# Four images on one core: where images 1 to 3 are loaded, normalised and laid out as a pixel table

## The chip, the cores and the metric

The kernel runs on one core of a Trainium2 chip. A core has a matrix engine (PE, whose weight loads are shown apart as PEld), a vector engine (DVE), an activation engine (ACT), a general engine (POOL) and a sequencer for transfers (SP). Each works through its own list of instructions in order and waits for the others by semaphores. Transfers (DMAs) are issued from the lists of SP, ACT and POOL; all share the core's 16 DMA engines. The metric is the time of one execution on the device in microseconds (us): 4742.62 us before the change, the median of three runs (4736.29 to 4742.63). All data are 32-bit floats.

## The reference, cut to what matters

The input `x` has four images of 32 by 32 pixels and 384 channels. Four layers follow each other, each a residual on a group-normalised input:

```python
x = x + _L0_conv_ref(_gn(x), ...)   # deformable attention, 6 heads of 64 channels
x = x + _L1_conv_ref(_gn(x), ...)   # attention, 12 heads of 32 channels, reweighted by a similarity
x = x + _L2_conv_ref(_gn(x))        # ratio of box sums
x = x + _L3_conv_ref(_gn(x), ...)   # outlook attention, 3 x 3 neighbourhoods
```

`_gn` takes the mean and variance of each image over groups of 12 channels and all 1024 pixels. Layer 0 projects the normalised image to queries, runs a grouped 3 x 3 convolution over them, turns its result into one sampling position for each pixel and head group, and samples the same normalised image bilinearly at these positions: four neighbouring pixels, weighted. The samples give keys and values; the logits also get a bias, sampled from a table around each position. No image depends on another.

## The kernel before

**Two lanes.** `Front` does layer 0 of an image, `Trunk` does layers 1 to 3. Image 0's front comes first, alone. Then the trunk of image b runs beside the front of image b + 1, and the trunk of image 3 runs alone. Both lanes are Python generators that emit instructions and yield a number of steps. `Net.layer3` mixes them: after each yield of the trunk it lets the front go on until its share is `LEAD` = 0.1 ahead of the trunk's. A trunk counts 1109 steps (`TRUNK_STEPS`), a front 714 (`FRONT_STEPS`). A front therefore ends when its trunk has done nine tenths, and the next front begins beside the last part of that trunk, the normalisation and products of its layer 3 (L1634 and on). A planner then puts the instructions of each engine in order from its own estimates of when each can start; what is emitted late can be placed early. Instructions under `pin` (`keep_in_program_order`) keep the order of the program.

**The first part of a front** is `normed(b)` (L544). It loads the image's pixels (`xin`, four DMAs of 384 KB on SP, L550), transposes them to channels on PE (24 transposes, L560) with eight copies on ACT (L565), stores the transposed image `x0` (one DMA of 1.5 MB on ACT's list, L568; `outputs0` reads it back at L457 for the residual), normalises it (`norm_steps`, L322: six statistics and three means on DVE, 28 one-column products with `gmat` on PE at L338, a square root on ACT at L361, three scalings on DVE at L369), transposes it back (24 transposes, L583; eight copies into `xn` on ACT, L589, two buffers) and stores every 128 pixels twice into the pixel table `pairs` in DRAM (16 DMAs of 192 KB on SP, L591), from which the bilinear samples are gathered (L707). `xin`, `x`, and the normalised `xh` share two buffers of one tag, `a12`. For image 0, `normed` also issues `borders` (L232, zeros at the edges of every pixel table, four DMAs for each on ACT's list) and `windows` (the bias tables, up to the six stores of `strips` at L193, also on ACT's list).

After `normed`, `inputs0` makes queries (`w_q`, 36 matmuls at L388, read back at L618), the convolution (216 matmuls, L637, read back at L645), layer norm and positions on DVE, the gathers and the keys and values. Then come the heads.

**Image 0's heads** (`heads0`) are a row of 96 blocks (6 heads, 2 halves of the queries, 8 key tiles) written out by hand as a software pipeline, with nearly everything pinned. A turn `t` runs from -3 to 118. Beside these turns the kernel already does one piece of another image: `early0` runs `normed(1)` and stores `xh` as `xh1` in DRAM. `normed(1)` yields in small pieces (30 in all, the flag `alone`), and one piece is taken after each turn from t = 17. So image 1's front starts from `xh1` and the finished table (L601 to L610), while images 2 and 3 call `normed` at the head of their own fronts, beside the trunks of images 0 and 1, in two lumps: up to the normalisation, and the pixel table.

**Buffers in DRAM**: two pixel tables and two `x0`, taken in turn by `b % 2`; one `xh1`.

Of the kernel before, what the change touches and what calls it, by code (L numbers as in the profile page):

```python
# [26 lines left out]
P = 128  # L27
NB, HW, C = 4, 32, 384
N = HW * HW
KC = C // P  # L30
NJ = N // P
G, GC = 6, 64
# [26 lines left out]

TRUNK_STEPS, FRONT_STEPS, LEAD = 1109.0, 714.0, 0.1


def bc(ap, axis, n):
# [7 lines left out]
class Net:  # L73
# [121 lines left out]
    def scratch(self):  # L195

        self.pairs = []
        for i in range(2):
            t = self.dram.tile([G * SLOTS, 2 * GC], F32, tag=f"pairs{i}", name=f"pairs{i}")
            self.pairs.append(t)  # L200
        dram = lambda name, shape: self.dram.tile(shape, F32, tag=name, name=name)

        self.x0 = [dram(f"x0_{i}", [C, N]) for i in range(2)]
        self.x1 = [dram(f"x1_{i}", [C, N]) for i in range(2)]

        self.qd, self.kd, self.xgd, self.yd = (dram(n, [C, N]) for n in ("qd", "kd", "xgd", "yd"))

        self.xh1 = dram("xh1", [C, N])
        self.k0 = dram("k0", [C, N])
        self.gcd = dram("gcd", [C, M1])  # L210
        self.vd = dram("vd", [N, C])

        self.den = [dram(f"den{h}", [1, N]) for h in range(G)]
        self.rden = [dram(f"rden{h}", [1, N]) for h in range(G)]
        self.lse = [dram(f"lse{p}", [2, N]) for p in range(NH1 // 2)]
        self.skew = [
            self.dram.tile([NJ, P * ROWP], F32, tag=f"skew{i}", name=f"skew{i}")
            for i in range(2)
        ]
# [191 lines left out]
class Front(Lane):  # L411
# [38 lines left out]
    def outputs0(self, b):  # L450
        nc, v = self.nc, self.nc.vector
        with self.scope("l0c"):
            w = self.weights("w_out")
            for ko in range(KC):
                rows = slice(ko * P, (ko + 1) * P)
                x = self.wt([P, N], "res", 2)
                nc.sync.dma_start(x, self.x0[b % 2][rows, :])  # L457
                ps = self.dense_t(w, self.qpad, ko)
                v.scalar_tensor_tensor(x, ps, self.col(C_BOUT, ko), x, ALU.add, ALU.add)
                nc.sync.dma_start(self.x1[b % 2][rows, :], x)  # L460
                yield 6
# [82 lines left out]
    def normed(self, b):  # L544

        nc = self.nc
        xin = self.wt([P, NJ, C], "a12", 2)
        src = self.a["x"][b].rearrange("(j p) c -> p j c", p=P)
        for j in range(0, NJ, 2):
            nc.sync.dma_start(xin[:, j : j + 2, :], src[:, j : j + 2, :])  # L550
        x = self.wt([P, KC, N], "a12", 2)

        alone = b == 1
        if alone:
            for _ in range(4):
                yield
        for j in range(NJ):
            ps = self.bank()
            for k in range(KC):
                nc.tensor.transpose(  # L560
                    ps[:, k * P : (k + 1) * P], xin[:, j, k * P : (k + 1) * P], self.ident
                )
            if alone:
                yield
            nc.scalar.copy(  # L565
                x[:, :, j * P : (j + 1) * P], ps[:, 0:C].rearrange("p (k n) -> p k n", k=KC)
            )
        nc.scalar.dma_start(self.x0[b % 2].rearrange("(k p) n -> p k n", p=P), x)  # L568
        xh = self.wt([P, KC, N], "a12", 2)
        for _ in self.norm_steps(x, xh):  # L570
            if alone:
                yield
        if b == 0:
            self.borders()
            self.windows()
        yield 25


        pv = self.pairs[b % 2].rearrange("(g s) (y c) -> y s g c", g=G, y=2)
        for j in range(NJ):  # L580
            ps = self.bank()
            for k in range(KC):
                nc.tensor.transpose(  # L583
                    ps[:, k * P : (k + 1) * P], xh[:, k, j * P : (j + 1) * P], self.ident
                )
            if alone:
                yield
            xn = self.wt([P, C], "xn", 2)
            nc.scalar.copy(xn, ps[:, 0:C])  # L589
            for y, first in ((0, HW + 1), (1, 1)):  # L590
                nc.sync.dma_start(  # L591
                    pv[y, first + j * P : first + (j + 1) * P],
                    xn.rearrange("p (g c) -> p g c", g=G),
                )
        return xh

    def early0(self):

        with self.scope("l0p"):
            xh = yield from self.normed(1)  # L600
            self.nc.sync.dma_start(self.xh1.rearrange("(k p) n -> p k n", p=P), xh)  # L601

    def inputs0(self, b):
        nc, v = self.nc, self.nc.vector
        pairs = self.pairs[b % 2]
        if b == 1:

            xh = self.wt([P, KC, N], "a12", 2)
            nc.sync.dma_start(xh, self.xh1.rearrange("(k p) n -> p k n", p=P))
            yield 25  # L610
        else:
            xh = yield from self.normed(b)
        yield 10
# [245 lines left out]
    def heads0(self, work):  # L859
# [3 lines left out]
        nc, v, pin = self.nc, self.nc.vector, self.tc.keep_in_program_order  # L863
        f, va = self.f, self.va
# [3 lines left out]
        n = len(blocks)  # L868
# [179 lines left out]
        other = self.early0()  # L1048
        for t in range(-3, n + OUT + 12):
            turn(t)  # L1050
            if t > 2 * NJ:
                next(other, None)
        yield 0

    def over_sums(self, k):
# [793 lines left out]
```

## Time and profile before

One execution was profiled. It took 4731.65 us, of which the span from the first to the last instruction is 4729.8 us. The median of the three timed runs, 4742.62 us, lies 11 us above it.

| what | from the profile |
|---|---|
| PE busy | 4165.4 us, 88% of the span |
| DVE busy | 3133.8 us, 66% |
| ACT busy | 2416.1 us, 51% |
| POOL busy | 945.7 us, 20% |
| DMA | 369.97 MB, 78 GB/s over the span |
| image 0's heads | about 205 to 570 us |
| three mixed stages (trunk 0, 1, 2 with front 1, 2, 3) | about 580 to 3920 us |
| image 3's trunk alone | about 3970 us to the end |

The profile gives for each engine the busy time, and for each group of instructions what ended the idle time before it. Busy time of PE is modelled at the end of each matmul, so it is not a measure of how close PE is to its peak. A stage is judged by the engine that is nearly always busy in it: elsewhere idle time costs nothing.

### The profile page before, as it was taken

The page shows a single profiled execution, that of the slowest core. Times are in us where ns is not written, and L with a number is a line of the kernel's source. Part 1 is how long each engine was busy: PE and PEld are TensorE (multiplying, and loading weights), DVE is VectorE, ACT ScalarE, POOL GpSimd, SP SyncE. Part 2 cuts the span into 40 slices and gives each one's busy share as a digit, 9 for nine tenths or more (in the row PEclk, how much of TensorE's full clock was granted, in tenths as well). Part 3 has the DMA queues.
Part 4 walks back from the last instruction along what each step waited for, and adds up shares of the span by engine and source line. Part 5 has one row for each costly group of instructions (what it writes and reads, how often), then busy time and mean ns, then how long its engine had stood idle before and what let it go on. Part 6 is the DMA issues. An engine that isn't in the chain of part 4 may idle for free. (4 is left out here: it accounts for less than half of the span.)

```text
span 4729.8 us, 46690 instructions
## 1 busy us (share of the span) xinstructions
PE 4165.4 (88%) x15704; PEld 1776.1 (38%) x15704; DVE 3133.8 (66%) x5772; ACT 2416.1 (51%) x3711; POOL 945.7 (20%) x946
## 2 busy tenths in 40 slices
PE   5477788999999988899899989899999999999988
PEld 2222233333333353333333444343333335343444
DVE  3599755777878727577877754767686874555544
ACT  2166433666666313566766332456675641556542
POOL 0533204221212103311212110421121211000000
PEclk8688888999999988999999989899999998999998
DMA  6435224221212143321212124431121213311011
GB/s 124 133 118 144 75 92 126 88 61 52 72 41 66 65 137 128 109 60 48 82 50 68 46 88 126 138 100 57 30 77 43 74 41 118 96 32 24 19 40 40
DMA packets 231727, 369.97 MB, mean 78 GB/s; under 512 B 117507, under 2 KB 164704, under 8 KB 231488
## 3 DMA queue, kind: packets, MB, share of 16 engines
q1 hardware_dynamic: 170472, 200.51, 14.3%
q0 software_dynamic: 39936, 145.53, 10.1%
q10 hardware_dynamic: 21080, 20.96, 1.8%
q8 instruction: 124, 2.03, 0.2%
q14 instruction: 115, 0.94, 0.1%
HBM read 287.41 MB, written 79.78 MB: 78 GB/s over the span
## 5 line engine op out<-in xcount | busy, mean ns | idle before, releaser
L1472 DVE SCALAR_TENSOR_TENSOR e<-bank,gam,e 128x512 f32<-128x512 f32 x768 | 558.4, 749 | 573.0 <-ACT gn L1471 276.8
L1463 PE MATMUL bank<-whole,sg 128*128 128x512 f32 (+3 forms) x2304 | 873.2, 513 | 2.5 <-DVE e L1472 2.5
L1323 ACT ACTIVATE big<-big,nmax 128x1024 f32<-128x1024 f32 x384 | 418.6, 1090 | 397.5 <-DVE nmax L1322 352.0
L1441 ACT ACTIVATE e<-big 128x1024 f32<-128x1024 f32 x384 | 376.9, 1019 | 360.4 <-PE big L1433 352.8
L1463 PEld LDWEIGHTS bank<-whole,sg 128*128 128x128 f32 x2304 | 406.5, 199 | 379.9 <-issue 301.7
L1322 DVE TENSOR_REDUCE nmax<-big 128x1 f32<-128x1024 f32 x384 | 453.0, 1218 | 62.0 <-PE big L1314 35.4
L792 POOL DMA_INDIRECT win<-strips,widx x288 | 307.1, 1066 | 634.0 <-DVE z L805 331.0
L1418 POOL TENSOR_SCALAR sg<-whole,gam 128x512 f32<-128x512 f32 x192 | 147.1, 769 | 1399.4 <-PE bank L1463 1139.5
L1433 PE MATMUL big<-qa,ka 64*128 64x512 f32 x1536 | 411.7, 627 | 14.7 <-ACT big L1323 8.9
L1314 PE MATMUL big<-k,q 32*128 32x512 f32 x1536 | 327.2, 690 | 74.7 <-ACT e L1441 35.3
L813 PE MATMUL bank<-qpad,kz 128*128 128x512 f32 x576 | 281.1, 614 | 15.0 <-DVE e L1472 15.0
L707 POOL DMA_INDIRECT gat<-pairs,sidx x192 | 210.0, 1094 | 418.0 <-DVE sidx L521 241.2
L848 PE MATMUL bank<-lg,va 128*64 128x512 f32 x576 | 265.4, 603 | 16.3 <-ACT lg L846 16.2
L848 PE MATMUL bank<-lg,ones 128*64 128x512 f32 x576 | 264.7, 602 | 0.0
L810 DVE SCALAR_TENSOR_TENSOR lg<-z,bias_f,lg 128x512 f32<-128x512 f32 x288 | 227.4, 802 | 39.3 <-ACT lg L809 37.1
L804 ACT ACTIVATE z<-win,bias_f 128x528 f32<-128x528 f32 x288 | 207.1, 739 | 63.1 <-DVE lg L810 40.0
L1433 PEld LDWEIGHTS big<-qa,ka 64*128 64x128 f32 x1536 | 134.7, 187 | 270.4 <-issue 153.9
L805 DVE SCALAR_TENSOR_TENSOR z<-win,bias_f,z 128x528 f32<-128x528 f32 x288 | 217.0, 772 | 27.4 <-DMA win<-strips,widx 16.4
L845 DVE TENSOR_TENSOR lg<-lg,tb 128x512 f32<-128x512 f32 x288 | 187.7, 705 | 52.3 <-ACT tb L838 51.5
L1407 PE MATMUL bank<-e,vs 128*32 128x512 f32 x1536 | 211.6, 607 | 2.1 <-DVE vs L1401 2.1
L809 ACT ACTIVATE lg<-z,bias_f 128x512 f32<-128x512 f32 x288 | 201.0, 720 | 18.3 <-PE bank L848 10.4
L814 DVE TENSOR_TENSOR lg<-bank,lg 128x512 f32<-128x512 f32 x288 | 192.4, 684 | 20.7 <-PE bank L813 18.4
(299 smaller groups left out, 6658.3 us busy)
## 6 DMA issues: line engine op xcount, KB each, us to landing
pairs<-xn SPq DMA_DIRECT2D x64, 192.0 KB
q<-qd SPq DMA_DIRECT2D x48, 256.0 KB
w<-in_gmat SPq DMA_DIRECT2D x16, 576.0 KB
w<-in_w_off SPq DMA_DIRECT2D x12, 576.0 KB
w<-in_Wqkv SPq DMA_DIRECT2D x12, 576.0 KB
a<-in_x SPq DMA_DIRECT2D x16, 384.0 KB
x<-a ACTq DMA_DIRECT2D x4, 1536.0 KB
win<-strips,widx POOLq DMA_INDIRECT x384
```

The source lines that it names most:

```text
L792: nc.gpsimd.indirect_dma_start(out=win, out_offset=None, in_=self.strips[:, :], in_offset=bass.IndirectOffsetOnAxis(ap=self.widx[:, q, c : ...
L805: v.scalar_tensor_tensor(z, wv[:, 1 : HH + 1, 0 : HW + 1], sc(0, 1), z, ALU.mult, ALU.add)
L810: v.scalar_tensor_tensor(lg, z[:, :, 1 : HW + 1], sc(0, 0), lg, ALU.mult, ALU.add)
L813: nc.tensor.matmul(ps, kz[:, j * P : (j + 1) * P], both, start=True, stop=True)
L848: nc.tensor.matmul(po[out, :], w, lf, start=j == 0, stop=j == NJ - 1)
L1314: nc.tensor.matmul(ps[r][:, h * 512 : (h + 1) * 512], self.q4[rows, i * P : (i + 1) * P], self.k4[rows, 0:512], start=True, stop=True,)
L1322: v.tensor_reduce(nmax[:, r, i : i + 1], ps[r], AX.X, ALU.max, negate=True)
L1323: nc.scalar.activation(ps[r], ps[r], AF.Exp, bias=nmax[:, r, i : i + 1], accum_out=den[:, r, i : i + 1],)
L1433: nc.tensor.matmul(ps[:, r, :], ka[rows, j * P : (j + 1) * P], qa[rows, cols], start=True, stop=True,)
L1441: nc.scalar.activation(e, ps, AF.Exp)
L1463: nc.tensor.matmul(ps[:, (mid - i0) * P :], sg[:, r, m, :], sim[:, r, m, mid * P : i1 * P], start=m == 0, stop=m == 1,)
L1472: v.scalar_tensor_tensor(e[:, r, :], ps, self.gam[:, 1:2], e[:, r, :], ALU.add, ALU.mult, accum_out=tot[:, r, h : h + 1],)
```

## The change

`early0` now runs `normed` for images 1, 2 and 3, one after the other, beside the heads of image 0, and takes its pieces from t = 1 on instead of t = 17. With 30 pieces for each image it needs 91 of the 118 turns from t = 1. Each normalised image is stored in its own `xh0[b]`; there are four pixel tables, four `x0`. Every later front begins with the load of `xh0[b]` in three DMAs of 512 KB and goes on to the queries. As `borders` zeroes the edges of all tables, it issues sixteen small DMAs in place of eight. A later front has 25 steps fewer, so `FRONT_STEPS` is 689.

```diff
-TRUNK_STEPS, FRONT_STEPS, LEAD = 1109.0, 714.0, 0.1
+TRUNK_STEPS, FRONT_STEPS, LEAD = 1109.0, 689.0, 0.1
@@ scratch
-        for i in range(2):
+        for i in range(NB):
             t = self.dram.tile([G * SLOTS, 2 * GC], F32, tag=f"pairs{i}", name=f"pairs{i}")
             self.pairs.append(t)
-        self.x0 = [dram(f"x0_{i}", [C, N]) for i in range(2)]
+        self.x0 = [dram(f"x0_{i}", [C, N]) for i in range(NB)]
-        self.xh1 = dram("xh1", [C, N])
+        self.xh0 = [dram(f"xh0_{i}", [C, N]) for i in range(NB)]
@@ outputs0
-                nc.sync.dma_start(x, self.x0[b % 2][rows, :])
+                nc.sync.dma_start(x, self.x0[b][rows, :])
@@ normed
-        alone = b == 1
+        alone = b > 0
...
-        nc.scalar.dma_start(self.x0[b % 2].rearrange("(k p) n -> p k n", p=P), x)
+        nc.scalar.dma_start(self.x0[b].rearrange("(k p) n -> p k n", p=P), x)
...
-        pv = self.pairs[b % 2].rearrange("(g s) (y c) -> y s g c", g=G, y=2)
+        pv = self.pairs[b].rearrange("(g s) (y c) -> y s g c", g=G, y=2)
@@ early0
-            xh = yield from self.normed(1)
-            self.nc.sync.dma_start(self.xh1.rearrange("(k p) n -> p k n", p=P), xh)
+            for b in range(1, NB):
+                xh = yield from self.normed(b)
+                self.nc.sync.dma_start(self.xh0[b].rearrange("(k p) n -> p k n", p=P), xh)
@@ inputs0
-        pairs = self.pairs[b % 2]
-        if b == 1:
+        pairs = self.pairs[b]
+        if b:
             xh = self.wt([P, KC, N], "a12", 2)
-            nc.sync.dma_start(xh, self.xh1.rearrange("(k p) n -> p k n", p=P))
-            yield 25
+            for k in range(KC):
+                nc.sync.dma_start(xh[:, k], self.xh0[b][k * P : (k + 1) * P, :])
@@ heads0
         for t in range(-3, n + OUT + 12):
             turn(t)
-            if t > 2 * NJ:
+            if t > 0:
                 next(other, None)
+        for _ in other:
+            pass
```

## The prediction

> **What bounds the kernel now.** I read the busy table first, then stages. PE is busy 88% of the span, so the mixed stages should follow PE; but the work is moved into the heads of image 0, so I asked for these alone. The table of stages has 30 turns with the pieces of `normed(1)` (turns 17 to 46), then 30 turns without them (47 to 76), then three times the last part of a trunk, from the square root of its layer 3 norm to the first copy of its transposes (L1745): trunk 0 with the first part of front 2 beside it, trunk 1 with that of front 3, and trunk 2 with none. Columns: stage, length, busy time and count for PE, PEld, DVE, ACT, POOL, then the granted clock, the DMA share and GB/s.
>
> ```profile
> 272.00:383.10 111.10, 88.64 (x283) 32.33 (x281) 104.99 (x168) 73.51 (x120) 39.66 (x33) 0.86 0.48 143
> 383.10:484.90 101.80, 78.20 (x204) 23.34 (x204) 100.72 (x155) 65.56 (x103) 40.57 (x34) 0.85 0.41 119
> 1655.00:1721.70 66.70, 52.54 (x238) 37.94 (x238) 21.39 (x53) 13.88 (x27) 1.81 (x2) 0.77 0.51 141
> 2787.70:2854.10 66.40, 52.91 (x238) 38.18 (x238) 21.38 (x53) 13.91 (x27) 1.89 (x2) 0.77 0.51 141
> 3924.20:3965.40 41.20, 35.06 (x151) 23.52 (x152) 14.25 (x36) 5.68 (x9) 0.00 (x0) 0.79 0.28 76
> ```
>
> In the heads DVE is busy 100.7 of 101.8 us: this stage is DVE's, and what is put on DVE there lengthens it. The same 30 turns took 9.3 us more with one image's normalisation among them. In the tail of a trunk nothing is full, yet with `normed` beside it the same trunk work took 66.7 and 66.4 us in place of 41.2: 25.3 us more. This stretch is a chain of short steps. PE's timeline shows where it goes; first trunk 0, then trunk 2:
>
> ```profile
> 1653.09 1.83 PE L338 MATMUL bank<-gn_d,w 128*128 128x1 f32 x14 [0.93 <-DVE gn_d L357]
> 1661.96 4.16 PE L560 MATMUL bank<-ident,a 128*128 128x128 f32 x24 [7.04 <-DMA a<-in_x]
> 1668.33 3.12 PE L338 MATMUL bank<-gn_mv,w 128*128 128x1 f32 x14 [2.21 <-issue]
> 1672.39 3.12 PE L338 MATMUL bank<-gn_d,w 128*128 128x1 f32 x14 [0.94 <-DVE gn_d L357]
> 1675.37 10.51 PE L402 MATMUL bank<-Wa,xh 128*128 128x81 f32 x48
> ```
> ```profile
> 3922.44 1.69 PE L338 MATMUL bank<-gn_d,w 128*128 128x1 f32 x14 [0.93 <-DVE gn_d L357]
> 3926.87 10.53 PE L402 MATMUL bank<-Wa,xh 128*128 128x81 f32 x48 [2.74 <-DVE xh L369]
> ```
>
> Columns: start, length, instruction, and in brackets the idle time before it and who ended it. In trunk 0 PE ends the layer 3 norm at 1654.92 us and begins that layer's products at 1675.37: 20.45 us later, the front's load, transposes and norm between. In trunk 2 the gap is 2.74 us. So 17.7 us of the 25.3 stand in one place.
>
> **The change part by part.**
>
> *Taken out of two tails* (images 2 and 3; image 1's `normed` is in the heads already). The gap of 17.7 us goes; the 24 transposes back (L583) go too, 3.4 us of PE in trunk 0's tail. Both lie on PE, which after the gap is idle only 7.7 us in the 115 until the next trunk's first `xp` (L1134), while queries, convolution and layer 3 fill it. Together 21.1 us for an image. The rest of the 25.3 us is `w_q` matmuls drawn forward and pixel-table stores ahead of `skew`, which I don't count. Upper bound 25.3 us. Lower bound: the front now needs 1.5 MB of `xh0` instead of 1.5 MB of pixels. If the planner puts the `w_q` matmuls before the layer 3 products, PE waits for it. The pixel load was issued at 1656.04 and its last transposes ended at 1666.12, so PE would stand some 11 us after 1654.92, and 10 us of the 21 remain. I take 21.1, since the `w_q` matmuls are emitted one trunk yield (30 steps) after the load, and those of front 1, loaded from DRAM in this way already, came behind the trunk's norm with no wait: 42.2 us for two images.
>
> A second view agrees in size. From the first `xp` copy of trunk 1 to that of trunk 2 (1789.24 to 2922.21) is 1133.0 us, from trunk 2 to trunk 3 (to 3998.72) 1076.5 us. The 56.5 us between are `normed`, `w_q` (36 matmuls, 16.1 us busy) and convolution (216, 26.3 us): at least 14 us for `normed`, and more by what the lone tail leaves idle (its rows fill 70.0 of 77.3 us).
>
> *Put into the heads.* For each image DVE gets six statistics (3.9 us), three means of them (0.6), five small steps (0.8) and three scalings (2.4): 7.7 us busy, and waits for PE (3.3) and ACT (1.3), in order before the pinned work. The 30 turns show 9.3 us net. PE's part (48 transposes 8.4 us, 28 products 4.4) and ACT's (16 copies 7.5 us, the root) fit beside: both have over 20 us idle in a hundred. SP gets 4 loads, 16 table stores, a `gmat` load and the `xh0` store per image, ACT's list one `x0` store; in turns 17 to 46 they made DVE wait nowhere (its only wait in a block is 0.5 us for ACT). If that cover were gone, each late store would stop ACT, as said below. The pieces fit: 91 of 118 turns. Image 1's pieces only start sixteen turns earlier, at the same price. `l0p`'s buffers now stay until about turn 91, near 550 us, where `res` (loaded at 389.82 before) can follow; it is used at 573.7, so nothing is late. Two images: 18.6 us; bounds 15.4 (DVE's busy time alone) and 24.6 (busy time and all waits).
>
> A square root among exponentials costs two table loads of 1.28 us per image on ACT (L361 and L995, one each). In the tail it cost none extra, as layer 3's norm loads the same table. ACT has 36 us idle in the 101.8, so I count nothing beyond the 9.3, which holds them.
>
> The Trainium skill (ScalarE: Activation LUTs, What ACT_TABLE_LOAD costs) speaks against this move: it prices each switch at 2.66 us with its drain, and its table of rules wants functions grouped by set. By that, as an estimate, four more switches take 10.6 us of ACT and, were ACT the limit, the sum below would end at -9.0 us. The trace shows 1.28 us for the load and no row for a drain.
>
> *Added at the start.* Eight more DMAs of zeros on ACT's list. Seven took 4.70 us there (29.50 to 34.20), so eight take 5.4 us. Behind them are `half`, two `xn` copies, the first `qpad` read-back (waits for PE until 40.47 anyhow) and six `strips` issues of 13.9 us, behind which PE waited 3.62 us for `xn`. Of the 5.4 us, those before 40.47 are partly covered by ACT's 4.95 us idle; but `strips` waits for `half`, now later. Bounds 0 and 5.4; I take 4, nearer the upper, as the chain `half` to `strips` has no slack visible.
>
> *Moved for nothing.* Four tables and four `x0` in place of two remove no wait that the trace shows. The three-part load of `xh0` moves the same bytes; front 1's load at 589.43 was needed at 601.55. The 25 steps less and 689 change when a front is emitted, not its work; its end stays at nine tenths of the trunk. I count 0, at most 3 us either way (half the idle time of PE in a hundred us of mixed stage, some 6).
>
> **Sum:** -42.2 + 18.6 + 4 = -19.6 us. The profiled 4731.65 becomes 4712; that execution lies 11 us under the median, and on the median's scale 4742.6 - 19.6 gives 4723. A measurement of this kernel tells about 0.2%, 9.5 us, from no change.
>
> **The rivals.**
>
> *PE waits for the new load in the tails* (about the same time). The wait for pixels is replaced by one for `xh0`: 10.1 us instead of 21.1 per image. -20.2 + 18.6 + 4 = +2.4, 4745. For it: the planner did put the front's transposes before layer 3's products, and PE stood 7.04 us. Against: 30 steps of trunk work lie between load and use.
>
> *SP's list stops ACT in the heads* (slower). The `xn` copies on ACT have two buffers, freed by stores on SP. SP stands for long times on the stores of the denominators, which wait for the end of a half:
>
> ```profile
> SPq L1025 <- ACT lg L1024: 130.8, 7, 27.6
> ```
>
> This is SP's view of waits in 410 to 560 us: total, times, longest. If the planner puts one table store behind such a wait, the next copy but one stops ACT, which is pinned ahead of DVE. One such stop costs up to 27.6 us: -19.6 + 27.6 = +8.0, 4751; two make 4778. It decides from 29 us of stops in all. Against: in turns 17 to 46 two such stores lay among the sixteen and ACT waited 0.4 us.
>
> *The tails give all of it* (faster still). 25.3 us twice, 7.7 us twice in the heads, no cost at the start: -50.6 + 15.4 = -35.2, 4707.
>
> **How the numbers follow.** Forecast 0.50, its own range 4710 to 4735 (the edits' bounds, partly cancelling); new load 0.18; SP 0.17; the full gain 0.15. Faster by over 9.5 us: nine tenths of the forecast, all of the last rival and little of the first, 0.62. The same: most of the first rival and the forecast's upper edge, 0.20. Slower: 0.18, SP's cases with a stop beyond 27.6 us and some of the first rival with the upper bounds in heads and start. The range reaches to the full gain with 3 us of pacing below it, 4704, and to one SP stop with the start's upper bound and the pacing, 4756; two stops and more are left out.
>
> **What would show it.** Right: the stretch from layer 3's root to L1745 falls from 66.5 us to near 45 (queries now inside it) in trunks 0 and 1; the gap before L402 falls to 3 us; the heads end some 20 to 25 us later than 568 us, DVE still over 95% busy, `normed`'s copies (L565, L589) all before 600 us. Wrong: PE waiting on `xh` in front of L388; ACT waiting on `pairs` stores in the heads; a turn with pieces that costs far more than 3.7 us; `strips` issued more than 6 us later; or a mixed stage that no longer fills PE once the front runs earlier.

## The result, and the profile after

The changed kernel is slower: 4751.16 us against 4737.99 us, medians of eight runs each (4744.39 to 4778.08, and 4729.14 to 4743.41). The ratio (of the means, as all ratios below) is 1.0038, 95% interval 1.0021 to 1.0055. Forecast were 4723 us and a gain of 19.6 us; the result lies 28 us above the forecast and on the other side of the kernel before, though inside the stated range of 4704 to 4756 us.

The profiled execution of the changed kernel took 4778.08 us, 27 us above the median of its runs, so its stages are set beside a second profile of the same kernel (run e6_after below, 4749.78 us).

The page of the changed kernel, its span and its busy table (busy time, share of the span, count of each engine):

```profile
span 4776.1 us, 46650 instructions
PE 4206.7 (88%) x15704; PEld 1775.4 (37%) x15704; DVE 3115.2 (65%) x5772; ACT 2429.9 (51%) x3721; POOL 935.2 (20%) x946
```

The same 15704 matmuls as before keep PE busy 41.3 us longer (4165.4 before), with DVE 18.6 us less. Nothing was added on PE, so it is busy longer on the same work; where, the stages must tell. (Busy time is the time in which at least one matmul's record runs. The records overlap, so it grows when matmuls get longer and also when they overlap less.)

The stages of the changed kernel that answer to the prediction's table: turns 17 to 46 and 47 to 76 of the heads, now both with pieces of `normed`, and the last part of trunks 0, 1 and 2 from the root of the layer 3 norm to L1745. Columns: stage, length, busy time and count of PE, PEld, DVE, ACT, POOL, granted clock, DMA share, GB/s.

```profile
280.70:393.60 112.90, 92.28 (x297) 35.45 (x295) 105.72 (x173) 73.87 (x121) 39.39 (x33) 0.83 0.55 162
393.60:506.40 112.80, 88.47 (x270) 31.43 (x266) 106.98 (x167) 73.43 (x121) 40.30 (x34) 0.83 0.55 166
1699.80:1761.60 61.80, 59.12 (x257) 33.05 (x258) 13.99 (x36) 10.27 (x13) 0.37 (x1) 0.86 0.34 106
2844.00:2905.50 61.50, 58.83 (x258) 32.91 (x259) 14.06 (x36) 10.31 (x14) 1.67 (x2) 0.86 0.35 108
3970.10:4012.20 42.10, 35.33 (x151) 23.72 (x152) 14.25 (x36) 5.66 (x8) 0.00 (x0) 0.79 0.31 80
```

A block of 30 turns with pieces takes 112.9 and 112.8 us (111.1 before, 101.8 without pieces). In the tails PE is now busy 59 of 62 us. They fall from 66.7 to 61.8 us only and not to the 45 us that was named as a sign, since PE fills the time with queries and convolution of the next front. PE's timeline in trunk 0's tail shows that the gap before the layer 3 products is gone (start, length, instruction, idle before it and who ended it):

```profile
1696.85 2.90 PE L338 MATMUL bank<-gn_d,w 128*128 128x1 f32 x14 [0.93 <-DVE gn_d L357]
1702.48 10.53 PE L402 MATMUL bank<-Wa,xh 128*128 128x81 f32 x48 [2.74 <-DVE xh L369]
```

It is 2.74 us, where it was 20.45 us with the front's work in it. So what the change aimed at happened. The loss is elsewhere. First the stages of the kernel before: the heads from 200 us to the first residual (L459), the whole of trunks 0 to 2 from the third `xp` copy (L1134) of image 0 to that of image 3, and in trunk 1 the stretch from its third `xp` copy to its first `sg` (L1418), then layer 1's first pair of heads:

```profile
200.00:573.70 373.70, 282.11 (x787) 96.30 (x786) 332.02 (x513) 215.30 (x340) 124.43 (x106) 0.84 0.38 112
664.00:4009.00 3345.00, 3052.71 (x11421) 1299.79 (x11420) 2324.03 (x4249) 1783.96 (x2745) 700.17 (x693) 0.94 0.26 79
1804.70:1920.90 116.20, 92.20 (x247) 36.84 (x245) 89.06 (x130) 48.08 (x77) 53.48 (x49) 0.82 0.50 157
1920.90:2055.00 134.10, 124.91 (x472) 54.34 (x472) 86.29 (x164) 71.08 (x112) 27.30 (x30) 0.97 0.32 93
```

The same four of the changed kernel (its heads from 205 us):

```profile
205.00:599.80 394.80, 305.37 (x939) 116.72 (x938) 345.46 (x547) 231.85 (x378) 123.45 (x106) 0.84 0.50 149
688.80:4055.20 3366.40, 3070.78 (x11269) 1278.75 (x11268) 2286.66 (x4211) 1777.24 (x2709) 690.47 (x693) 0.93 0.25 75
1818.00:1955.80 137.80, 102.63 (x263) 40.80 (x261) 88.82 (x133) 45.34 (x73) 50.02 (x48) 0.76 0.42 134
1955.80:2098.20 142.40, 134.35 (x499) 55.46 (x501) 97.20 (x181) 82.69 (x130) 30.87 (x34) 0.99 0.32 91
```

Trunks 0 to 2 have 152 matmuls fewer on PE (the transposes and norm products of two images) and yet PE is busy 18 us longer, and the stretch is 21.4 us longer rather than 42.2 us shorter. In trunk 1 the first stretch grew by 21.6 us and the next by 8.3. They hold the front's gathers and its first heads. (`big` and `bank` in the lines below are the tiles that PE writes its products to.) Image 3's trunk, alone, stayed the same: 720.8 us before, 720.9 after.

Below, a trunk is cut in two: its *body* from the third `xp` copy to the root of the layer 3 norm, its *tail* from there to the next trunk's third `xp` copy.

| us | first residual | body 0, 1, 2 | tail 0, 1, 2 |
|---|---|---|---|
| before | 573.7 | 992.3, 984.2, 987.8 | 148.5, 148.7, 83.5 |
| after | 599.8 | 1012.3, 1027.3, 1010.4 | 116.9, 115.7, 83.8 |

The tails gave 64.6 us, more than was forecast, and the bodies took 85.7 back. In the bodies no work was added. What differs there is when the front's instructions are emitted: without the 25 steps, and with `FRONT_STEPS` 689.

### The profile page after: what moved, and what is told of

It is laid out like the page before. It is cut to its first block, busy times and chain, and to the rows that moved or that the text cites. A ratio compares the mean times of both kernels' runs of the same rounds, so it can differ in the third digit from the quotient of the medians.

```text
span 4776.1 us, 46650 instructions
## 1 busy us (share of the span) xinstructions
PE 4206.7 (88%) x15704; PEld 1775.4 (37%) x15704; DVE 3115.2 (65%) x5772; ACT 2429.9 (51%) x3721; POOL 935.2 (20%) x946
## 4 chain that ended last, share of the span: by engine, by line
PE 53%; DVE 20%; ACT 14%; issue 6%; DMA 3%; POOL 3%; ACTq 1%; another core or an unknown queue 0%; SPq 0%; DVEq 0%; POOLq 0%
PE bank L1466 10%; PE big L1436 5%; PE bank L402 4%; PE bank L814 4%; PE big L1317 4%; PE big L388 4%; PE bank L849 3%; PE bank L1410 3%; PE bank L1461 3%; ACT big L1326 3%; DVE nmax L1325 2%; POOL gat L708 2%; DVE e L1475 2%; PE big L638 2%; ACT whole L1363 1%
## 5 line engine op out<-in xcount | busy, mean ns | idle before, releaser
L1466 PE MATMUL bank<-whole,sg 128*128 128x512 f32 (+3 forms) x2304 | 863.2, 509 | 0.0
L1325 DVE TENSOR_REDUCE nmax<-big 128x1 f32<-128x1024 f32 x384 | 453.8, 1219 | 48.3 <-PE big L1317 28.2
L814 PE MATMUL bank<-qpad,kz 128*128 128x512 f32 x576 | 300.4, 646 | 16.7 <-DVE e L1475 16.7
L708 POOL DMA_INDIRECT gat<-pairs,sidx x192 | 206.0, 1073 | 355.0 <-DVE sidx L521 199.1
L811 DVE SCALAR_TENSOR_TENSOR lg<-z,bias_f,lg 128x512 f32<-128x512 f32 x288 | 213.4, 756 | 46.2 <-ACT lg L810 43.7
```

Of the source, the lines that this page charges most:

```text
L708: nc.gpsimd.indirect_dma_start(out=gat[:, g].rearrange("p l c -> p (l c)"), out_offset=None, in_=pairs[:, :], in_offset=bass.IndirectOffse ...
L814: nc.tensor.matmul(ps, kz[:, j * P : (j + 1) * P], both, start=True, stop=True)
L1325: v.tensor_reduce(nmax[:, r, i : i + 1], ps[r], AX.X, ALU.max, negate=True)
L1466: nc.tensor.matmul(ps[:, (mid - i0) * P :], sg[:, r, m, :], sim[:, r, m, mid * P : i1 * P], start=m == 0, stop=m == 1,)
```

## The experiments

All ratios are to the kernel before on the same chip, with 95% intervals. The runs were made in four groups, each on one chip of its own beside the kernel before, which has medians there of 4704.78 (e1, e2, e3, e5), 4708.57 (e4, e6, e7, e8), 4705.67 (e9 to e12) and 4708.5 us (e13 to e16); in the first comparison it was 4737.99 us. Line numbers shift by a few lines between kernels. Diffs are against the changed kernel unless another is named.

**Theory P: the pace.** The loss comes from the places at which the later fronts are emitted. **Rival M: the moved work** and its traffic, in the heads or in DRAM. e1 gives the changed kernel its old pace back; e2 changes the pace of the kernel before and moves nothing; e5 does the heads' and the start's part alone.

e1_pace:

```diff
-TRUNK_STEPS, FRONT_STEPS, LEAD = 1109.0, 689.0, 0.1
+TRUNK_STEPS, FRONT_STEPS, LEAD = 1109.0, 714.0, 0.1
@@ inputs0, after the three loads of xh0[b]
+            yield 25
```

> The changed kernel, with 25 steps yielded after the load of xh0 and FRONT_STEPS back at 714, so that each later front is emitted at the same trunk steps as before the change. Theory (pace): the trunks' bodies, from the third xp copy to the root of layer 3's norm, return from 1011, 1026 and 1009 us to about the 991, 983 and 986 of before; start and heads still cost 26, the two tails still give 50 to 64; time 4738 + 26 - 50 = about 4710, between 4700 and 4722. Rival (the moved work itself, by other DRAM places or a lower clock): the bodies stay 20 to 40 us longer and the time stays near 4750.

Measured 4678.90 us, ratio 0.9944 (0.9928 to 0.9961): 25.9 us faster than the kernel before.

e2_pace_only (against the kernel before):

```diff
-TRUNK_STEPS, FRONT_STEPS, LEAD = 1109.0, 714.0, 0.1
+TRUNK_STEPS, FRONT_STEPS, LEAD = 1109.0, 689.0, 0.1
@@ normed
-        yield 25
+        yield 0 if b > 1 else 25
@@ inputs0, after the load of xh1
-            yield 25
```

> The kernel before, with only the pace of the changed one: FRONT_STEPS 689 and no 25 steps after the load or the normalisation of a later front. Normalisation stays in the tails. Theory (pace): slower than before by what the three bodies lost, 60 to 86 us, so 4798 to 4824; the DVE wait for the gathers at the weighing line appears, some 18 us in each trunk. Rival (the moved work itself): no change, 4738 within 10.

Measured 4782.80 us, 1.0164 (1.0147 to 1.0181): the pace alone costs the kernel before 78.0 us, though nothing is added to the program (its profile has six more table loads on ACT, 174 against 168, and the same counts on PE, DVE and POOL).

e5_twice (images 2 and 3 are normalised in the heads and again in their fronts):

```diff
+TRUNK_STEPS, FRONT_STEPS, LEAD = 1109.0, 714.0, 0.1
-    def normed(self, b):
+    def normed(self, b, alone=False):
...
-        alone = b > 0
@@ early0
-                xh = yield from self.normed(b)
+                xh = yield from self.normed(b, True)
@@ inputs0
-        if b:
+        if b == 1:
...
+            yield 25
```

> The heads' part alone: at the pace of before, images 1 to 3 are normalised beside the heads as in the changed kernel, but images 2 and 3 are then loaded, normalised and laid out once more at the head of their own fronts. Theory (heads and start cost 26 us and nothing else of the move costs): 4738 + 26 = 4764, the bodies as before, the tails as before (66 us). Rival (the move also slows the mixed stages): 4780 or more.

Measured 4724.26 us, 1.0044 (1.0027 to 1.0060): the heads' and the start's part costs 19.5 us (12.7 to 28.2). So M falls: the moved work costs what it was priced at, and taking it out of the tails (e5 to e1) gives 45.4 us. The windows of the stretch over trunks 0 to 2 say the same. First e5, then e1, then e2:

```profile
688.40:4000.60 3312.20, 3037.61 (x11421) 1294.17 (x11420) 2321.78 (x4249) 1783.81 (x2746) 702.82 (x693) 0.94 0.27 80
```
```profile
686.00:3953.80 3267.80, 3016.14 (x11269) 1271.84 (x11269) 2308.79 (x4215) 1769.92 (x2711) 704.87 (x693) 0.95 0.26 77
```
```profile
664.90:4064.00 3399.10, 3091.85 (x11422) 1304.95 (x11421) 2300.21 (x4245) 1792.54 (x2744) 696.89 (x693) 0.93 0.26 78
```

From e5 to e1 the stretch falls by 44.4 us with 152 matmuls fewer; e2, with e5's matmuls within one record, needs 86.9 us more than e5: 54.2 of it PE busy longer on them, 32.7 PE idle.

**The zeros at the start.** e3 issues the zeros of tables 1 to 3 later, from SP, each ahead of its `normed`; e4 does this to e1.

```diff
-    def borders(self):
+    def borders(self, images=range(1)):
...
-        for t in self.pairs:
+        for t in [self.pairs[i] for i in images]:
...
-                nc.scalar.dma_start(v[first:last, :, y, :], bc(zero[0 : last - first], 1, G))
+                eng.dma_start(v[first:last, :, y, :], bc(zero[0 : last - first], 1, G))
@@ early0
             for b in range(1, NB):
+                self.borders(range(b, b + 1))
```

> The changed kernel, but the zeros at the edges of the tables of images 1 to 3 are issued from SP beside the heads, ahead of each image's normalisation, and only image 0's four at the start on ACT. Theory (the start's zeros lie on the path): the first weighing of image 0 comes back from 129 to near 120 us, some 8 us sooner than in the changed kernel, and the time falls by 5 to 9 us to about 4744. Rival (hidden or lost in the mixed stages): 4751 as the changed kernel.

> Both mends together: the pace of before (25 steps after the load of xh0, FRONT_STEPS 714) and the zeros of the later tables issued from SP beside the heads. Theory: the two add up, 0.9944 less 4 to 5 us of 4705, so 0.993 of before. Rival (the start's 5 us are lost again further on): 0.9944.

Measured: e3 4743.41 us, 1.0088 (1.0071 to 1.0104), beside 1.0070 of the changed kernel; e4 4679.23 us, 0.9939 (0.9914 to 0.9963), beside 0.9944 of e1. The first weighing of samples (L721) begins at 126.3 (e3) and 125.5 us (e4), against 129.1 in the changed kernel and 123.9 before. In e1, where all sixteen are issued at the start, it begins at 126.9. So the later zeros bring back 2.8 us (e3 against the changed kernel) or 1.4 us (e4 against e1) at the start, less than the 8 us expected of e3, and nothing that can be told apart in the time.

**What in the pace.** e6 is the changed kernel once more:

> The changed kernel itself once more, beside the others of this group. On the chip of the first group the kernel before took 4704.8 and the changed one with late zeros 1.0088 of before. Expected: 1.009 to 1.011 of before, that is 1.0088 and the 4 to 5 us of the zeros. If it is 1.004, as first measured, late zeros cost time in place of saving it.

Measured 4747.59 us, 1.0070 (1.0049 to 1.0091). In the first comparison the change cost 13.2 us (1.0038), here 39.0; the intervals overlap only from 1.0049 to 1.0055, and e1 and e2 have no run beside the first comparison. What the pace costs there may be less than it measured here. e6's stretch over trunks 0 to 2, and the two stages of trunk 1 (as above):

```profile
691.00:4022.80 3331.80, 3048.56 (x11269) 1273.07 (x11269) 2285.30 (x4211) 1777.12 (x2709) 696.13 (x693) 0.94 0.25 76
1810.30:1934.80 124.50, 97.46 (x263) 39.91 (x263) 88.14 (x133) 45.16 (x74) 53.14 (x49) 0.81 0.47 148
1934.80:2078.30 143.50, 136.39 (x499) 56.08 (x499) 97.28 (x181) 82.95 (x130) 31.07 (x33) 0.96 0.31 91
```

And the two stages of e1:

```profile
1786.90:1894.90 108.00, 90.55 (x247) 35.90 (x247) 88.55 (x130) 48.17 (x78) 53.38 (x48) 0.85 0.55 171
1894.90:2031.50 136.60, 126.83 (x470) 55.29 (x471) 86.44 (x164) 70.95 (x111) 28.04 (x29) 0.96 0.31 90
```

Over the same 11269 matmuls e6 needs 64.0 us more than e1: 32.4 us of longer busy time (3048.56 - 3016.14) and 31.6 us of more idle time of PE (283.2 against 251.7). The halves are those of this pair alone: against e7 below, of e6's own chip, the 64.7 us are 48.9 and 15.8. PE's waits in the whole stretch, first e6, then e1 (waiting line, released by: total, times, longest):

```profile
PE big L1317 <- ACT big L1326: 53.4, 34, 3.2
PE bank L735 <- DVE xn L724: 41.8, 11, 7.2
PE bank L849 <- ACT lg L847: 25.9, 29, 2.6
PE big L1317 <- ACT e L1444: 19.5, 23, 2.2
```
```profile
PE big L1318 <- ACT big L1327: 35.7, 21, 3.3
PE big L1318 <- ACT e L1445: 34.7, 29, 2.4
PE bank L850 <- ACT lg L848: 16.2, 24, 1.6
PE bank L736 <- DVE xn L725: 11.9, 3, 4.0
```

The largest difference is PE's wait for the weighed samples (`xn`, L724 and L725): 41.8 against 11.9 us. DVE, which weighs them, waited for the gathers 19 times and 91.3 us over the whole changed kernel in its first profile (21 times and 93.9 us in e6), 12 times and 43.5 us in e1. That gives two theories. **G: the gathers.** The front's inputs now come 25 steps earlier after its start, and DVE stands in order at gathers that haven't landed, as POOL issues the 48 of an image in a row at 1.25 us each (0.95 us busy, 0.30 between). **H: the heads' place.** What counts is where the heads' blocks fall among the trunk's rows. e7 keeps the inputs early and puts the 25 steps, empty, between inputs and heads, so that the heads fall as before; e8 halves the gathers.

e7_mid:

```diff
-TRUNK_STEPS, FRONT_STEPS, LEAD = 1109.0, 689.0, 0.1
+TRUNK_STEPS, FRONT_STEPS, LEAD = 1109.0, 714.0, 0.1
@@ at the end of the later fronts' inputs
         yield 30
+        if b:
+            yield 25
```

> The changed kernel with FRONT_STEPS 714 and the 25 empty steps put between a later front's inputs and its heads: the inputs are emitted early as in the changed kernel, the heads at the steps of before. Theory A (early inputs are the loss: the gathers, 1.25 us each on POOL, are waited for on DVE in front of the trunk's own inputs): the stretch from the third xp copy to the first sg stays at 120 to 130 us and pair 0 at 143, DVE waits some 90 us in all for gathers, the last stretch (first sg of pair 4 to layer 3's root) returns from 355 to 347; ratio about 1.003. Theory B (the heads' pace is the loss): bodies near 980 us, ratio near 0.995.

e8_half (the later fronts leave out half of the bilinear samples: three groups of six are gathered and weighed in two halves):

```diff
-            for g in range(G):
+            for g in range(G // 2 if b else G):
...
+            if b:
+                return weigh_half(j, gat)
```

> The changed kernel, later fronts gathering only three of the six groups of each 128 pixels; the weighing is done in two halves on the same three groups, so DVE's work stays nearly the same and POOL's gathers halve. It leaves half of the bilinear samples out. Theory A (DVE stands in order for gathers that POOL issues at 1.25 us each, 60 us for an image): DVE's waits for gathers, 91 us in all, fall below 20, the stretch before the first sg falls from 124 to about 108 us in each of three trunks, ratio lower than the changed kernel's by 0.8% or more. Theory B (heads' pace): the waits go but the bodies stay above 1000 us, ratio within 0.3% of the changed kernel's.

Measured: e7 4681.72 us, 0.9939 (0.9916 to 0.9963), as fast as e1; e8 4715.71 us, 1.0012 (1.0000 to 1.0024), 32 us below the changed kernel. Windows over trunks 0 to 2, e7, then e8:

```profile
688.70:3955.80 3267.10, 2999.70 (x11269) 1272.13 (x11268) 2296.50 (x4211) 1759.32 (x2699) 699.37 (x693) 0.95 0.26 77
```
```profile
691.70:3993.10 3301.40, 3054.42 (x11269) 1276.40 (x11268) 2292.31 (x4283) 1777.57 (x2710) 622.24 (x621) 0.94 0.25 74
```

e8's 0.6% lies between what its two theories forecast (0.8% or more, at most 0.3%). Halved gathers take the idle time away (247.0 us, as in e1) but not the longer busy time (3054.4 us). So the waits for samples stand behind the idle half of e6's loss, but not behind the other half. And e7, whose inputs are as early as the changed kernel's, loses nothing: with the heads later (27 trunk steps, by the table below) the trunk makes it good, its first stretch in trunk 0 at 145.2 us and its first pair at 101.1 (128.5 and 144.8 in the changed kernel). G fails as the cause; H stands, but one could still say that only the speed of the front matters (76 or 73 front steps beside one pair of layer 1's heads), not its place. e9 has e1's speed with the 25 empty steps at the front's end, so that inputs and heads both come early; e10 halves the gathers at e1's place; e11 gives 50 empty steps ahead of the heads; e12 starts the changed kernel's fronts later, at its own speed.

```diff
@@ e9_end: FRONT_STEPS 714, at the end of a front
             yield from self.outputs0(b)
+            yield 25
@@ e10_half_pace: e8's halved gathers in e1 (half of the samples left out)
@@ e11_mid50: FRONT_STEPS 739, at the end of the later fronts' inputs
+        if b:
+            yield 50
@@ e12_lead
-TRUNK_STEPS, FRONT_STEPS, LEAD = 1109.0, 689.0, 0.1
+TRUNK_STEPS, FRONT_STEPS, LEAD = 1109.0, 689.0, 0.065
```

> The changed kernel with FRONT_STEPS 714 and the 25 empty steps at the very end of a later front. A pair of the trunk (118 steps) then has 118 x 714 / 1109 = 76.0 front steps beside it, which is one whole head (two halves of 38), as before the change; with 689 it is 73.3. But the heads begin as early as in the changed kernel and end earlier. Theory 1 (pace: one head beside one pair): bodies near 980 us, ratio 0.994 to 0.997. Theory 2 (the early begin itself): bodies above 1000 us, ratio 1.003 or more.

> The control for the halved gathers: the pace of before (as in the first mended kernel, 0.9944) and only three of six groups gathered in later fronts, so half of the bilinear samples is left out. If waiting for gathers is a loss of the changed pace alone, halving saves at most 8 us here: 0.993. If gathers are waited for at any pace, it saves the 0.6% that it saved in the changed kernel: 0.988.

> FRONT_STEPS 739 with 50 empty steps between the inputs and the heads of a later front: heads begin later still and go faster, 78.6 front steps beside a pair. Theory 1 (76 steps, one head beside one pair, is what counts): slower than with 25 by 10 us or more, ratio 0.996 to 1.003. Theory 2 (the later the heads the better): 0.993 or less.

> The changed kernel with LEAD 0.065 in place of 0.1: everything of a later front comes 39 trunk steps later, its heads begin about where they did before the change, but at 73.3 front steps beside a pair. Theory 1 (pace): bodies stay above 1000 us and the ratio near the changed kernel's 1.007. Theory 2 (the early begin itself): bodies near 980 us, ratio about 0.995.

Measured: e9 4748.86 us, 1.0091 (1.0073 to 1.0108); e10 4687.97, 0.9964 (0.9949 to 0.9978); e11 4732.79, 1.0061 (1.0044 to 1.0079); e12 4782.66, 1.0168 (1.0147 to 1.0190). The speed of e1 without its place is as slow as the changed kernel (e9). In the good place halved gathers gain nothing (e10). More room ahead of the heads (e11) and a later front (e12) do not help either; both are slower than any theory forecast for them. They have another speed as well, so they don't part place from speed; e16 below does, at e1's speed. e9's window over trunks 0 to 2:

```profile
691.90:4028.00 3336.10, 3013.38 (x11269) 1278.36 (x11268) 2274.16 (x4211) 1749.36 (x2690) 698.49 (x693) 0.94 0.25 76
```

It is 68.3 us longer than e1's. PE is busy as long as there (3013.4 and 3016.1 us); what grew is its idle time (322.7 against 251.7 us). So a bad place can cost idle time alone, and e6's halves are no rule.

**How sharp, and does it repeat?** At speed 714 a pair of layer 1's heads (118 trunk steps) stands beside 118 x 714 / 1109 = 76.0 front steps, which is one head of the front (two halves of 38), and a row of the trunk (14 steps) beside 9.0, three blocks of 3. At 689 it is 73.3 and 8.7. If H is right and the halves of the heads count, moving all by half a head, 38 x 1109 / 714 = 59.0 trunk steps, should give the heads a good place again, and a shift of less should not. In the expectations P now stands for the place within a pair. All four are e1 with the heads at another place:

```diff
@@ e13_lead153
+TRUNK_STEPS, FRONT_STEPS, LEAD = 1109.0, 714.0, 0.1532
@@ e14_lead127
+TRUNK_STEPS, FRONT_STEPS, LEAD = 1109.0, 714.0, 0.1266
@@ e16_lead090
+TRUNK_STEPS, FRONT_STEPS, LEAD = 1109.0, 714.0, 0.09
@@ e15_mid12: in place of e1's 25 steps, 12 ahead of the heads and 13 at the front's end
```

> The mended pace (25 steps after the load, FRONT_STEPS 714) with LEAD 0.1532 in place of 0.1: everything of a later front comes 59 trunk steps earlier, which is the length of one half of a head, so the halves stand at the same places within the trunk's pairs as before, one half sooner. Theory P (the place within a pair counts): ratio 0.994 to 0.998, the stretch from pair 4 to layer 3's root 347 to 350 us. Theory Q (only the one tuned place is good, earlier is worse by as much as it is early): ratio 1.010 or more.

> The same with LEAD 0.1266: 29.5 trunk steps earlier, half of one half. Theory P: the worst place, ratio 1.005 or more, bodies above 1000 us. Theory Q: between the mended pace and LEAD 0.1532.

> Inputs early as in the changed kernel, 12 empty steps before the heads and 13 at the end, FRONT_STEPS 714: heads 20 trunk steps earlier than with 25 before them (0.994), 19 later than with none (1.009). Theory P and Q alike: between these two, near 1.002; if it is below 0.997 or above 1.006, the time turns on single rows of a pair and not on a broad place.

> The mended pace with LEAD 0.09: everything 11 trunk steps later, less than one row of a pair (14). Theory P: the place is nearly the same, ratio 0.994 to 0.998. If it is above 1.002, a single row decides.

Measured, in one table with the others. The place is the trunk step, counted from the first pair, at which the heads begin; it is worked out from the constants: heads begin when the trunk's share plus `LEAD` reaches 234/714 in e1, at step (0.3277 - 0.1) x 1109 = 253, and the first pair begins at step 173. The third column is the place's rest within half a head at that speed (59.0 steps at 714; 61.2 at 689, 57.0 at 739).

| kernel | place | rest | ratio | 95% interval |
|---|---|---|---|---|
| e1, 714 | 79.6 | 20.6 | 0.9944 | 0.9928 to 0.9961 |
| e4, 714 | 79.6 | 20.6 | 0.9939 | 0.9914 to 0.9963 |
| e7, 714 | 79.6 | 20.6 | 0.9939 | 0.9916 to 0.9963 |
| e13, 714 | 20.6 | 20.6 | 0.9997 | 0.9985 to 1.0009 |
| e16, 714 | 90.6 | 31.6 | 1.0083 | 1.0058 to 1.0107 |
| e9, 714 | 40.7 | 40.7 | 1.0091 | 1.0073 to 1.0108 |
| e14, 714 | 50.1 | 50.1 | 1.0134 | 1.0110 to 1.0159 |
| e15, 714 | 59.4 | 0.4 | 1.0113 | 1.0091 to 1.0136 |
| e11, 739 | 104.8 | 47.8 | 1.0061 | 1.0044 to 1.0079 |
| changed kernel (e6), 689 | 52.5 | 52.5 | 1.0070 | 1.0049 to 1.0091 |
| e12, 689 | 91.3 | 30.1 | 1.0168 | 1.0147 to 1.0190 |

The kernel before has the place 79.6 too. At speed 714 a rest of 20.6 is good at place 79.6 and less so at place 20.6, and each of the four other rests that were tried costs 1.4 to 1.9% against e1. e16 lies 11 trunk steps from e1, less than one row of 14, and is 1.4% slower (0.9944 to 1.0083), 65 us of 4705. e15, expected between e1 and e9, is not faster than e9. e13 is half a head earlier: its 0.9997 lies between the forecasts of P (0.994 to 0.998) and Q (1.010 or more), nearer to P. It is 0.9 to 1.4% better than its neighbours e9, e15 and e14; its bodies of trunks 1 and 2 (981.4 and 975.1 us) are as e1's (981.3 and 979.7), and only trunk 0's (1006.3 against 979.7) is longer. Its windows over trunks 0 to 2, then e14's:

```profile
690.40:3981.50 3291.10, 2981.37 (x11269) 1256.51 (x11268) 2286.46 (x4213) 1762.43 (x2702) 696.83 (x693) 0.95 0.26 77
```
```profile
689.00:4042.60 3353.60, 3064.09 (x11269) 1280.19 (x11268) 2292.62 (x4211) 1762.81 (x2694) 694.74 (x693) 0.94 0.25 75
```

PE's busy time on the same matmuls goes from 2981 to 3064 us with nothing but the start of the fronts moved by 30 trunk steps.

What stays open is the last step: which instruction behind which makes a place good. The period of half a head rests on one repeat, e13. The rival that is left is the planner: it puts the instructions in order anew for every place, so that the time could jump with any shift, whether heads and rows fit or not. No run parts the two. No single wait follows the time: PE's wait for samples is 41.8 us in e6 but 12.5 in the profile of the changed kernel that took 34.6 us longer over these trunks, and 16.5 in e12. What a slow run loses are many short waits, in each run other ones, and in most of them PE is also busy longer. Five of the 59 places were tried at speed 714; whether another beats 20.6 is open.

The best versions measured are e1, e4 and e7, at 0.994 of the kernel before and about 0.987 of the changed kernel (0.9944 / 1.0070 for e1, whose runs are of another chip than e6's; 4679.23 / 4747.59 = 0.986 for e4 on the same chip; 0.9944 / 1.0038 = 0.991 by the first comparison). They are the change with the old pace.

## Why the prediction was wrong

*The step that failed* is the one that counted the pace at nothing: "The 25 steps less and 689 change when a front is emitted, not its work; its end stays at nine tenths of the trunk. I count 0, at most 3 us either way". It is true that no work changes. It measured 78.0 us on the kernel before (e2) and 68.4 us on the change (4747.59 to 4679.23, e6 to e4, the late zeros included). The bound of 3 us came from half of PE's idle time in a hundred microseconds, as though a front could be early or late once; but the ratio and the offset hold all through a trunk, in three trunks, and cost 21 us in each (64.0 from e1 to e6). Also, the bound looked at idle time only, and half of that loss is no idle time at all: PE is busy longer on the same matmuls. That 4751 us lies inside the stated range is luck: its upper end stands on a stop of SP's list, which did not come.

*The tails*, 42.2 us: right. From e5 to e1 the time falls by 45.4 us, the stretch over trunks 0 to 2 by 44.4. The gap before L402 fell to 2.74 us, as forecast. The tail alone gives 27.8 and 26.3 us (149.0 and 148.4 in e5, 121.2 and 122.1 in e1), above the upper bound of 25.3, and the bodies of e1 give back 9.3 us in all (979.7, 981.3, 979.7 against 979.2, 977.9, 974.3): what was drawn forward, `w_q` and convolution, does count, and is partly repaid. One figure of the second view, rows that fill 70.0 of 77.3 us, adds up rows that overlap; PE was busy 67.4 us there.

*Heads and start*, 18.6 + 4 us: right. e5 measured 19.5 us for both (12.7 to 28.2). In the profile of the changed kernel the first weighing is 5.2 us later (123.9 to 129.1; forecast 4, upper bound 5.4), and the heads take 20.9 us more (26.1 us to the first residual less these 5.2), within 15.4 to 24.6. In e1 the first weighing is only 3.0 us later. A turn with pieces took 3.76 us, as expected of 3.7. The fifteen zeros on ACT's list took 9.49 us where seven took 4.70 (changed kernel, ACT's timeline):

```profile
29.54 9.49 ACTq L232 DMA_DIRECT2D pairs<-zero  x15
41.72 17.95 ACTq L193 DMA_DIRECT2D strips<-half  x6
```

*The table loads* on ACT: the trace's side held. L361 has 16 loads where it had 14 and L996 four where it had two, still 1283 ns each, and ACT's busy time in the heads rose by 16.6 us (215.3 to 231.9), with DVE 345.5 of 394.8 us still the fuller engine. The Trainium skill's price with the drain (ScalarE: Activation LUTs, What ACT_TABLE_LOAD costs) would have made heads and start 33.2 us, were ACT the limit, as an estimate; e5's interval ends at 28.2.

*The rival of SP's list* fell. ACT's waits in the heads of the changed kernel (215 to 560 us) have for the `xn` copies behind table stores

```profile
ACT xn L589 <- DMA pairs<-xn: 5.5, 4, 2.0
```

5.5 us in four times, the longest 2.0, far from the 29 us at which it decides. *The rival of the new load* fell too: PE never waits for the loaded `xh` in a tail. *The full gain* did not come either: e1, with the pace kept, stands at -25.9 us (0.9928 to 0.9961: -33.9 to -18.4), between the -19.6 of the sum and the -35.2 of that rival.

So the sum was right for the change with its pace kept, within the interval, and the result is that sum with the pace's cost on top. Measured apart, the parts do not add up: e1's -25.9 and e2's 78.0 make 52.1 us, and the change cost 39.0 (e6) and 13.2 (first comparison). The prediction's last sign, "a mixed stage that no longer fills PE once the front runs earlier", was the one that came: PE idles 31.6 us more in e6 than in e1, which is one half of the loss. It had no price in the sum.

## What to carry to other kernels

Where two streams of instructions are interleaved on engines that work in order, the ratio and the offset of the streams are a part of the schedule: when a change takes steps out of one, keep its pace first (empty steps do), measure, and only then tune the pace as an edit of its own. Ask of a pacing constant whether its two periods fit (here 76 front steps beside a pair of 118 trunk steps, two halves of 38) and try a shift by a fraction of the period. The fit alone is not enough: e9, e14, e15 and e16 have it and lose, and a shift of less than one row was worth 1.4%. In a stage that is full an edit that changes no work can still cost time, and its cost is to be counted for every repeat of the pattern.

## What the runs showed of the hardware that was not expected

*The same matmuls keep PE busy for different times.* Over the same 11269 matmuls PE's busy time ranges from 2981 us (e13) over 3016 (e1) to 3064 us (e14), and the granted clock from 0.95 to 0.94. The matmuls' own records hardly change from e1 to e6 (their mean is 554.5 and 555.4 ns); they overlap less. From e13 to e14 the mean grows by 1.0% (548.9 to 554.3 ns) and the busy time by 2.8%. In trunk 1's stretch with the gathers the clock is 0.85 in e1, 0.81 in e6 and 0.76 in the profile of the changed kernel. The waits of that stretch in e6 and in e1:

```profile
PE bank L735 <- DVE xn L724: 14.7, 4, 7.2
PE big L1317 <- ACT big L1326: 6.5, 4, 2.7
```
```profile
PE bank L1164 <- DVE qk L1174: 5.9, 1, 5.9
PE bank L736 <- DVE xn L725: 4.0, 1, 4.0
PE big L1318 <- ACT big L1327: 3.5, 2, 2.6
```

So a stop of PE can be paid for twice, as a wait and as a lower clock behind it. The Trainium skill (TensorE: Matmul & The Clock Gate, What's actually happening) has a rule for it: the clock is either full or half, and half after about 3.4 us of idling. The clock records of these traces hold the same two values, half of it in periods that are multiples of 3.41 us. But short stops are enough here: in e1's stretch 52 of the 58 periods at half clock begin with no single idle time of PE of 3.4 us in the 6.8 us before them, 34 with none of 2 us (idle time by the modelled ends of the matmuls).

Half clock adds up to 355.0 us of e1's stretch and 385.7 us of e6's, summed from the clock records. The 30.7 us more lose at most 15.4 us, if PE is busy in all of them: half of the 32.4 us. The clock is therefore not the whole of it. What makes the matmuls overlap less in the rest of the time was not shown by a run; stops that are shorter than a record would not be seen as idle time. Nor does the sum of idle time set the clock: e13 has the least time at half clock (331.1 us) with 309.7 us of idle time, more than e6.

*The six stores of `strips` took 17.95 us to issue*, where they took 13.90 us before. It looks as if the zeros ahead of them, 0.63 us each, delayed them, but they do not: in e3, with only image 0's zeros ahead of them, they took 16.90 us (ACT's timeline), and 16.43 us in e1 with all sixteen.

```profile
28.89 2.08 ACTq L234 DMA_DIRECT2D pairs<-zero  x3
34.99 16.90 ACTq L193 DMA_DIRECT2D strips<-half  x6
```

Both kernels with two pixel tables (before and e2) took 13.90 and 14.16 us, and those with four 16.43 us and more; why is open.
